# Layer 3's end: the last batch's chain woven with priority over the shared expert's rows and the first dense units

## The chip, the core and the metric

The kernel runs on one core of a Trainium2 chip. The metric is the device time of one execution in microseconds. The core's engines each work through a queue of their own, in order: TensorE (PE, matmuls), VectorE (DVE), ScalarE (ACT), GpSimd (POOL) and SyncE (SP, which only issues DMAs).

## What is computed

The reference is a decoder of four layers on x of shape (4, 512, 128), float32. Each layer adds a self-attention, a cross-attention and a feed-forward block to x, each with a layer norm before it. The change is in the last block, layer 3's mixture of experts:

```python
X = x.reshape(-1, D)                      # x after the layer norm, D = 128
scores = jax.nn.sigmoid(X @ gate_w.T)     # 32 experts
_, idx = jax.lax.top_k(scores + bias[None, :], K)          # K = 4
w = take(scores, idx); w = w / clip(sum(w), 1e-12)
pos = ...                                 # how many earlier tokens chose this expert
valid = pos < C                           # capacity of an expert, C = 128 over all 2048 tokens
h = silu(xe @ W1) * (xe @ W3); ye = h @ W2                 # per expert
out = sum over k of ye * w                # the dropped ones count 0
out = out + silu(X @ sw1.T) * (X @ sw3.T) @ sw2.T          # the shared expert
```

(Shortened here; in the reference C is worked out as 2 * T * K // E with T = 512, E = 32, which is 128. The kernel keeps one running count of choices over the four batches.)

## The kernel before

Tokens lie 128 to a tile, four tiles to a batch of 512. `x` holds the sum so far by rows, `xn` the normed rows, and `xT` the normed tokens turned, so that a batch is a 128x512 operand.

The kernel is written as Python generators whose steps are woven together by `Net.weave(dense, chain, every)`: after so many steps of the one, a step of the other is written. A planner then orders the instructions of each engine: among those that are ready, the one written first goes first. `high_priority(offset=n)` ranks the instructions written under it as if they had been written n places earlier. Stretches under `manual_schedule` keep the written order on the engines named. Tiles of one tag share a ring of buffers; in this stage TensorE writes into PSUM banks of the tags `f` (four), `acc` (one) and `s` (three).

The end of layer 3 goes like this. Batches 0 to 2 are routed during the cross-attention: their tokens are scattered into slots of their experts in DRAM by GpSimd's indirect DMAs (`put`, with a `pause` between two). Batch 3 is done in another way, densely: all experts see all its tokens. When the cross-attention is over, `add_columns(3)` adds its last sum onto x, and the stage of the change begins. It weaves two things:

- The dense side: `shared_rows` of batches 0, 1 and 2, two steps each. The first step writes the gate and the up product into two `f` banks (64 rows by 512), takes the silu on ScalarE (line 932) and the product on VectorE; the second step writes the down product into an `f` bank and adds it to x. After these come the first five steps of `dense_rows(3)`, which are units of experts for batch 3: gate and up products from `x3` into two `f` banks, silu (line 1065), product.
- The chain of batch 3: `norm(3)` (statistics and a reciprocal root on VectorE, lines 475 to 499; scaling on ScalarE, line 501; turning on TensorE, line 525; the copy to xT on ScalarE, line 526), `tokens_in_three` (xT as a sum of three bfloat16 parts, `x3`: a cast on ScalarE, line 732, the rest `x_rest` on VectorE, a second cast, line 735, and a difference), and `route_dense`, which is `capped` (router products and a sigmoid, line 594; the top four with max and match_replace; sums of weights; `before`, the counts of earlier choices; the places, lines 721 and 724) and then the weights split in three and turned into `w3T` (lines 747 to 756).

`w3T` is read by `weighted`, from the sixth dense step on. `widened` casts three packs of weights from bfloat16 to float32 (`w_wide`, lines 437 and 439); these are written before the weave. `slot_experts` follows: it fetches the slots of batches 0 to 2 from DRAM by eight DMAs on SP, computes the experts, and scatters the results back by 32 indirect DMAs on GpSimd. `returned` fetches these rows and adds them to x, and `store` writes the output.

In the stage before this one, the chains of batches 0 to 2 are woven with `ahead=300`; there, `weave` writes each step of a chain under `high_priority(offset=300)` until a step says "later".

Of the kernel before, what the change touches and what calls it, by code (L numbers as in the profile page):

```python
# [2340 lines left out]
def chained(*chains):  # L2341
    for c in chains:
        yield from c


def some(steps, n):

    for _ in range(n):
        if next(steps, steps) is steps:
            return  # L2350
        yield


def build(nc, packs, dram):
# [16 lines left out]
    with tile.TileContext(nc) as tc, ExitStack() as ctx:  # L2371
        net = Net(ctx, tc, packs, dram, feed)
# [96 lines left out]
        dense = lambda b: net.l2_dense(b, y[b], w4, s4)  # L2469
# [56 lines left out]
        shared = [net.shared_rows(b, net.stay[of("l3_ffn")[0]], ff) for b in range(3)]  # L2526
        chain = chained(net.norm(3), net.tokens_in_three(3, ff), net.route_dense(3, W5, s5))

        dense = net.dense_rows(3, ff)
        net.weave(chained(*shared, some(dense, 5)), chain, 0.3)  # L2530
        with tc.manual_schedule(engines={mybir.EngineType.Pool}):
            net.weave(net.slot_experts(at["l3"], ff), some(dense, 9), 3, 4)
        with tc.manual_schedule(engines={mybir.EngineType.DVE}):
# [28 lines left out]
```

## Time and profile before

| | us |
|---|---|
| median of 4 runs | 2147.36 |
| lowest and highest | 2143.18, 2151.99 |
| the profiled execution | 2143.46 |
| its span, first to last instruction | 2140.9 |
| TensorE busy | 2029.1 (95%) |
| VectorE, ScalarE, GpSimd busy | 1593.3, 989.6, 594.0 |
| mean granted TensorE clock | 0.984 |

Every time in a line of the profile is counted from the start of the span. A line of the timeline gives start, duration, engine, line of the code and operation with its output and inputs; in brackets stands how long the engine was idle before it and what released it. L431 is `dot` and L442 is `tt`, helpers through which most products and most two-operand steps of VectorE go; what they belong to is seen by the tile they write. The chain of waits is followed back from the last instruction, at each step to what released it. The granted clock is the share of its full speed that TensorE was allowed.

### The profile page before, as it was taken

Reading aid. Unit: us, or ns where it says so; the run is one execution under the profiler, and the core shown is the slowest. Engines: PE = TensorE matmul, PEld = TensorE weight load, DVE = VectorE, ACT = ScalarE, POOL = GpSimd, SP = SyncE. Lnnn points to the kernel's source line nnn. Section 1 sums busy time; section 2 is a strip of 40 time slices with the busy share of each in tenths; the row PEclk is TensorE's granted clock in tenths of the full one; section 3 lists DMA queues with packets and bytes.
Section 4 is the critical chain, followed back from the end, with each engine's and each line's share of the span. In section 5 each row is a group of like instructions: output and inputs, shape, how many; then the busy total and the mean of one; then the engine's idle time right before and its main releaser. Section 6 shows DMA issues by size and latency. Waiting matters only on the chain.

```text
span 2140.9 us, 27766 instructions
## 1 busy us (share of the span) xinstructions
PE 2029.1 (95%) x8804; PEld 1065.3 (50%) x8804; DVE 1593.3 (74%) x3932; ACT 989.6 (46%) x2023; POOL 594.0 (28%) x778
## 2 busy tenths in 40 slices
PE   6989999999999999999999999999999999899886
PEld 3556546554545453444444544444444444466553
DVE  6788665756775779788977798777866877599754
ACT  4566546444325462544543454434433544267541
POOL 2110001000000001433333243332433355245753
PEclk8999999999999999999999999999999999999998
DMA  6421443344453343343333444444454354431112
GB/s 162 122 78 47 107 113 101 93 130 112 118 137 89 93 105 99 89 104 97 102 103 106 111 112 127 123 134 115 127 135 119 98 141 124 96 99 36 32 43 82
DMA packets 93985, 222.56 MB, mean 104 GB/s; under 512 B 22178, under 2 KB 43106, under 8 KB 93582
## 3 DMA queue, kind: packets, MB, share of 16 engines
q1 hardware_dynamic: 90702, 218.63, 38.1%
q0 software_dynamic: 3136, 2.16, 0.4%
q8 instruction: 69, 1.13, 0.2%
q14 instruction: 78, 0.64, 0.1%
HBM read 192.55 MB, written 23.53 MB: 101 GB/s over the span
## 4 chain that ended last, share of the span: by engine, by line
PE 60%; DVE 13%; ACT 3%; issue 3%; POOL 2%; DMA 1%; another core or an unknown queue 0%; SPq 0%; DVEq 0%; POOLq 0%; ACTq 0%
PE mm L431 17%; PE f L431 11%; PE mm L1874 8%; PE s L431 6%; PE mm L1846 5%; PE acc L1039 5%; PE mm L1821 4%; DVE h L442 1%; DVE at_m L1907 1%; ACT at_e L1909 1%; DVE gvx L442 1%; PE acc L2326 1%; DVE k_work L442 1%; DVE og L442 1%; DVE x L442 1%
## 5 line engine op out<-in xcount | busy, mean ns | idle before, releaser
L1782 POOL TENSOR_TENSOR gvx<-gvx 128x512 f32<-128x512 f32 (+1 forms) x256 | 262.7, 1026 | 530.1 <-DVE gvx L442 471.7
L431 PE MATMUL f<-xT,w_l_ffn 128*128 128x512 f32 (+1 forms) x700 | 334.9, 599 | 1.3 <-ACT h L1031 0.7
L1909 ACT ACTIVATE at_e<-mm,at_m 128x512 f32<-128x512 f32 x256 | 173.1, 686 | 265.0 <-DVE at_m L1907 259.6
L431 PE MATMUL mm<-w_l_ffn_qkv,xT 128*128 128x512 f32 x512 | 264.4, 602 | 3.3 <-DVE gvx L442 1.7
L1874 PE MATMUL mm<-og,w_l_ffn_o 128*128 128x512 f32 x512 | 263.2, 600 | 2.8 <-DVE og L442 1.4
L442 DVE TENSOR_TENSOR h<-h,f 128x512 f32<-128x512 f32 (+1 forms) x175 | 119.4, 684 | 121.8 <-PE f L431 94.3
L1031 ACT ACTIVATE h<-f 128x512 f32<-128x512 f32 x172 | 102.2, 596 | 210.7 <-PE f L431 187.1
L442 DVE TENSOR_TENSOR gvx<-mm,gv 128x512 f32<-128x512 f32 x256 | 174.2, 684 | 23.7 <-PE mm L431 19.8
L442 DVE TENSOR_TENSOR og<-mm,c 128x512 f32<-128x512 f32 x256 | 174.1, 682 | 22.8 <-PE mm L1874 20.9
L431 PEld LDWEIGHTS f<-xT,w_l_ffn 128*128 128x128 f32 (+1 forms) x700 | 125.7, 190 | 130.2 <-issue 107.2
L1039 PE MATMUL acc<-h,w_l_ffn 128*128 128x512 f32 x344 | 176.7, 597 | 4.2 <-DVE h L442 2.9
L1907 DVE TENSOR_REDUCE at_m<-mm 128x1 f32<-128x512 f32 x256 | 161.2, 682 | 11.8 <-PE mm L431 11.2
L1822 ACT COPY eT<-mm 128x512 f32<-128x512 f32 x256 | 137.3, 595 | 68.4 <-PE mm L1821 68.0
L1821 PEld LDWEIGHTS mm<-ident,at_e 128*128 128x128 f32 x1024 | 119.4, 141 | 66.5 <-issue 45.4
L1874 PEld LDWEIGHTS mm<-og,w_l_ffn_o 128*128 128x128 f32 x512 | 91.3, 190 | 114.6 <-issue 90.7
L1821 PE MATMUL mm<-ident,at_e 128*128 128x128 f32 x1024 | 134.8, 273 | 3.3 <-ACT at_e L1909 3.3
L431 PEld LDWEIGHTS mm<-w_l_ffn_qkv,xT 128*128 128x128 f32 x512 | 86.9, 190 | 91.5 <-issue 54.5
L431 PE MATMUL mm<-roped 64*128 64x512 f32 x512 | 129.4, 615 | 1.6 <-DVE roped L442 1.6
L1846 PE MATMUL mm<-eT,v 128*64 128x512 f32 x512 | 118.5, 599 | 2.1 <-ACT eT L1822 2.1
L442 DVE TENSOR_TENSOR h<-h,c 128x512 f32<-128x512 f32 x160 | 111.1, 700 | 3.4 <-DMA c<-l_ffn_w 0.4
L1248 ACT ACTIVATE e<-mm 128x512 f32<-128x512 f32 (+1 forms) x176 | 92.1, 554 | 42.9 <-PE mm L1244 39.1
L1202 DVE TENSOR_REDUCE m<-mm 128x1 f32<-128x512 f32 (+3 forms) x176 | 102.7, 625 | 11.9 <-PE mm L1198 11.2
(528 smaller groups left out, 3481.4 us busy)
## 6 DMA issues: line engine op xcount, KB each, us to landing
c<-gates SPq DMA_DIRECT2D x256, 256.0 KB
c<-l_ffn_w SPq DMA_DIRECT2D x96, 384.0 KB
w_l_ffn_qkv<-in_l_ffn_qkv SPq DMA_DIRECT2D x24, 640.0 KB
w_l_ffn<-in_l_ffn SPq DMA_DIRECT2D x26, 576.0 KB
w_l_ffn_o<-in_l_ffn_o SPq DMA_DIRECT2D x24, 512.0 KB
rot<-qk SPq DMA_DIRECT2D x128, 64.0 KB
d<-inverted SPq DMA_DIRECT2D x64, 128.0 KB
k_parts<-k SPq DMA_DIRECT2D x12, 384.0 KB
```

The source lines that it names most:

```text
L431: self.nc.tensor.matmul(out, lhsT=lhsT, rhs=rhs, start=i == 0, stop=i == len(pairs) - 1)
L442: self.nc.vector.tensor_tensor(out, a, b, op)
L1031: nc.scalar.activation(h, pg, AF.Silu)
L1039: nc.tensor.matmul(acc["t"], lhsT=W["d" + u], rhs=h, start=i == 0, stop=i == n - 1)
L1202: nc.vector.tensor_reduce(m[:, i, h0 : h0 + per], ps, AX.X, ALU.max, negate=True)
L1782: nc.gpsimd.tensor_tensor(x[:, :, :m], x[:, :, :m], x[:, :, m : 2 * m], ALU.add)
L1821: nc.tensor.transpose(p[:, j, :], es[i][hl][:, j * P : j * P + P], self.ident)
L1822: nc.scalar.copy(eT[hl][:, :, i * P : i * P + P], p)
L1846: nc.tensor.matmul(po[64 * hl : 64 * hl + 64, :], lhsT=m["v"][:, j, hl, :], rhs=eT[hl][:, j, :], start=j == 0, stop=j == TB - 1,)
L1874: nc.tensor.matmul(acc, lhsT=W["o"][:, (e - 1) * D : e * D], rhs=hs.pop(e - 1), start=e == 1, stop=e == E)
L1907: nc.vector.tensor_reduce(m, s, AX.X, ALU.max, negate=True)
L1909: nc.scalar.activation(e[:, :n], s, AF.Exp, bias=m, accum_out=den)
```

## The change

One call gets one more argument:

```diff
         chain = chained(net.norm(3), net.tokens_in_three(3, ff), net.route_dense(3, W5, s5))
 
         dense = net.dense_rows(3, ff)
-        net.weave(chained(*shared, some(dense, 5)), chain, 0.3)
+        net.weave(chained(*shared, some(dense, 5)), chain, 0.3, ahead=300)
```

What `weave` does with it:

```python
while due >= every:
    with self.tc.high_priority(offset=ahead) if ahead and urgent else ExitStack():
        urgent = next(chain, None) != "later"
    due -= every
```

None of the steps of this chain says "later", so all steps that are written inside the loop over the dense side are ranked 300 places earlier. At 0.3, more than three steps of the chain are written after each step of the dense side. Instructions, operands and DMAs are the same as before; only their order on the engines can differ.

## The prediction

> **What bounds the kernel now.** I read the page first. TensorE is busy nearly all the time, and the chain that ended last runs through it.
>
> ```profile
> span 2140.9 us, 27766 instructions
> PE 2029.1 (95%) x8804; PEld 1065.3 (50%) x8804; DVE 1593.3 (74%) x3932; ACT 989.6 (46%) x2023; POOL 594.0 (28%) x778
> PE 60%; DVE 13%; ACT 3%; issue 3%; POOL 2%; DMA 1%; another core or an unknown queue 0%; SPq 0%; DVEq 0%; POOLq 0%; ACTq 0%
> ```
>
> That is an average over many stages. The change touches only the 29.4 us between the copy of the last attention sum (ends 2031.93) and the first slot product (2061.36), so I read the chain of waits there, in order of time (start, us, what):
>
> ```profile
> 2032.64 1.86 PE f L431 x4
> 2034.50 2.74 issue
> ...
> 2039.13 1.05 PE f L431 x2
> ...
> 2042.39 0.70 DVE x_rest L442
> 2043.73 5.67 PE f L431 x12
> 2049.40 2.02 PE s L431 x14
> ```
>
> Two things stand out. First, TensorE idles 2.74 us from 2034.50, although batch 1's gate product (tokens and weights long there) needs nothing from the norm; it starts only at 2039.06, after batch 0's down products. So the rows of the shared expert are a serial string, gate and up, silu, multiply, down, then the next batch, as they take the f banks in program order; the first dense unit (2052.96) follows batch 2's down. Second, from 2040.2 to 2043.73 the string waits for ScalarE and VectorE (the x_rest line is the last of that wait). The timeline of ScalarE there:
>
> ```profile
> 2040.20 0.59 ACT L526 COPY xT<-s 128x512 f32<-128x512 f32 x1 [1.87 <-PE f L431]
> 2040.69 1.16 ACT L439 CAST w_wide<-w_l_ffn 128x1152 f32<-128x1152 bf16 x1
> 2041.74 0.62 ACT L732 CAST x<-xT 128x512 bf16<-128x512 f32 x1
> 2042.26 0.59 ACT L932 ACTIVATE h<-f 64x512 f32<-64x512 f32 x1
> 2042.87 1.28 ACT L594 ACT_TABLE_LOAD   x1
> 2044.16 0.28 ACT L594 ACTIVATE sig<-s 128x128 f32<-128x128 f32 x1
> ```
>
> Batch 1's silu (L932) is ready at 2040.2 and runs at 2042.26, just ahead of the router's sigmoid. Third view: the stretches of 3.41 us (start:end, length, then busy time and count of PE, PEld, DVE, ACT, POOL; then PE clock):
>
> ```profile
> 2043.27:2046.69 3.42, 2.96 (x10) 2.12 (x11) 2.48 (x9) 2.94 (x4) 3.05 (x6) 0.50 0.01 0
> 2046.69:2050.10 3.41, 3.41 (x8) 1.18 (x6) 2.34 (x14) 0.59 (x1) 2.21 (x5) 0.50 0.03 3
> 2050.10:2053.51 3.41, 3.41 (x25) 2.85 (x25) 1.84 (x9) 0.00 (x0) 0.00 (x0) 1.00 0.63 189
> 2053.51:2056.92 3.41, 3.41 (x10) 1.25 (x8) 1.79 (x6) 0.90 (x2) 0.00 (x0) 0.50 0.99 355
> ```
>
> The granted clock is whole or half and changes on this grid. Half windows follow windows of idling or of many narrow products (the places' 128x32).
>
> **The change, part by part.** Nothing is added or removed; no DMA is issued by the moved steps. Every step of batch 3's chain (norm, three-part tokens, router, top four, places, turned weights) is put 300 places earlier in the planner's ranking, so wherever one of its instructions is ready it goes ahead of the shared rows, the weight casts (w_wide) and the dense units.
>
> What the chain's speed is worth: little. Its last product, w3T, is written at 2058.04 and first read at 2068.72; x3 is complete at 2045.77 and first read at 2052.96. Those 10.7 and 7.2 us of cover stand, so an earlier chain earns nothing itself. Norm on VectorE already runs without a foreign instruction between (2033.40 to 2036.65): zero there, and the 2.74 us stall stays. Pool has one memset of the chain and no other work of it; its queue is untouched. The slot fetches, on SP behind Pool's last scatter (2049.15), land by 2057.3: 4 us before their first reader, which covers a shift to earlier of that size.
>
> What it costs: places in the queues. ScalarE is a strict line. After xT (ends 2040.79) the ranking now prefers the cast to x (0.62, ends 2041.41). The shared silu stays behind the cast w_wide, which is ranked ahead of it as before (1.16, 2042.57). By then the second cast is ready (x_rest takes 0.69 from 2041.41), and so is the sigmoid, as the gate products (1.08) no longer wait for batch 1's up product. So: second cast 0.61 to 2043.18, table load 1.28, sigmoid 0.28 to 2044.74, table load back 1.28, silu 0.59 to 2046.61. Before, the silu ended at 2042.85: 3.76 later. The attention stage, where the other batches' chains have this same 300, shows such a double load: 1.28 at 2009.84, sigmoid 0.28, 1.28 at 2011.43, with the exponential behind them.
>
> The Trainium skill (ScalarE: Activation LUTs, What ACT_TABLE_LOAD costs) puts a switch at 2.66 us, 1.28 of load and 1.38 of drain. The rows show the 1.28 and no drain: the silu ends at 2042.85, the load starts at 2042.87, the sigmoid 0.01 after it. With the page's price the silu would be 2.8 later still; I go by the rows.
>
> VectorE's multiply (0.68) then meets the top four and the counts (sigmoid's sum to the last of them: about 3.7 us of work from 2044.74, so to 2048.5). It ends between 2047.29, if it finds a gap at once, and 2049.2, if it goes last. I take 2047.7, nearer the first, since those instructions depend on one another and leave gaps; before it ended at 2043.68. So 4.0 us later, and TensorE waits meanwhile: behind the missing down product, in the banks' order, stand batch 2's products and all dense units.
>
> From there TensorE works without a break. Before: 2043.73 to 2052.96, of which 6.37 at half clock, that is 3.19 + 2.86 = 6.05 us at full clock; then the dense units and w3T's turns to 2061.36, 0.55 + 1.70 + 4.44 = 6.69 at full clock. After, from 2047.7: half clock to 2050.10, since the window before is nearly empty (1.20 done, 4.85 left). If the next window is full, the dense units start at 2054.95, else at 2056.66. They end 6.69 later, or 1.70 more with one half window: 2061.64, 2063.34, 2063.35, 2065.05. Against 2061.36 that is +0.3, +2.0, +2.0, +3.7. I take +2.0.
>
> The Trainium skill (TensorE: Matmul & The Clock Gate, Part 1) says that about 3.4 us without work halves the clock and one busy window restores it; it warns of such gaps, and the change lengthens one. But 2050.10:2053.51 is busy throughout and is followed by a half window, so here products of little width count as idling. By the page alone the window after 2050.10 would be full and the sum +0.3.
>
> Behind 2061.36 everything moves along: slots, Pool's 32 scatters (1.27 us apart, none waited for at the end), the last products, the adds. One cover is uncertain: the chain of waits has three stalls of unknown origin there.
>
> ```profile
> 2091.19 4.23 another core or an unknown queue
> ...
> 2104.46 3.04 another core or an unknown queue
> 2107.66 2.67 another core or an unknown queue
> ```
>
> They sum to 9.9 us, more than any term above; they may grow or shrink by some us.
>
> The profiled execution took 2143.46 us (span 2140.9 and 2.6 around it), 3.9 below the median of the runs, 2147.36. +2.0 makes it 2145.5; on the median, 2149.4.
>
> **The rivals.** *The silu keeps its place* (0.25). If the gate products or the second cast are not ready when w_wide ends, batch 1's silu slips in as before. For it: sigmoid and silu now stand only one instruction apart. Then only the adds into x (0.69) and a multiply leave the chain's way, and nobody waits for the chain: -0.5. At best the gaps close and both groups of half windows vanish: 3.4 + 1.7 of half clock and the 1.73 wait at 2042.0, together -6.8.
>
> *The shared rows starve* (0.25), the slower side. If the multiply goes behind the last count, it ends at 2049.2. TensorE has done 0.45 by 2050.10; with two half windows (1.70 each) the remaining 2.2 end at 2059.1, the dense units at 2065.8 or, with one more half window, 2067.5: +4.4 to +6.1. Batch 2's multiply then meets the split of the weights (1.07): +6.5 in all. It decides from the point where the chain leaves no gap on VectorE; two parallel strings, counts and sums, speak for it, their waits for one another against it.
>
> *Absorbed later* (0.08): the three stalls shrink by what is lost: 0.
>
> **How the numbers follow.** Forecast 0.42: +2.0, 2149.4 us. A gap of 0.3% (6.4 us) is about what a measurement of this kernel can tell from no change. The forecast's own range, +0.3 to +3.7, stays within it; only the stalls or the spread of runs (2143.18 to 2151.99) carry it out. Slower by more: some 0.6 of the starving case, 0.2 of the forecast's: 0.25. Faster by more: a quarter of the silu case and a little of the rest: 0.10. Within: 0.65. The range takes -6 to +9.5 about the median: 2141.5 to 2157.
>
> **What would show it.** Right: sigmoid's table load before batch 1's silu on ScalarE; TensorE idle for 4 us or more about 2043 to 2047; x3 and w3T finished earlier; the first dense product later than 2052.96. Wrong: the silu still ahead of the sigmoid, or fewer half windows between 2037 and 2061, or batch 1's gate product starting before batch 0's down, which would break the serial string and make the stage shorter.

## The result and the profile after

The changed kernel takes 2153.15 us (median of 52 runs, 2142.76 to 2161.62) against 2147.38 us (78 runs, 2133.59 to 2158.55). The ratio of the runs is 1.0023, with a 95% interval of 1.0015 to 1.0032: about 5 us slower (3.2 to 6.9); the two medians are 5.8 us apart. The ratio lies within the 0.3% that the prediction set as its bound, though its interval reaches just beyond, and it is more than the +2.0 us forecast. In the experiments below, one of the twelve runs of `shared_too` took 3474.53 us, far above all others, and is not in its ratio.

The profiled execution of the changed kernel took 2162.78 us (span 2161.1), 9.6 us above its median, so it is not to be subtracted as a whole from the one before. It enters the stretch in question late: the copy of the last attention sum ends at 2042.30, 10.4 us later than before, in code that the change does not touch. Two lines of the page and its chain that ended last:

```profile
span 2161.1 us, 27767 instructions
PE 2046.1 (95%) x8804; PEld 1072.8 (50%) x8804; DVE 1592.8 (74%) x3932; ACT 989.8 (46%) x2023; POOL 592.7 (27%) x778
...
PE 60%; DVE 13%; ACT 3%; issue 3%; POOL 1%; DMA 1%; another core or an unknown queue 1%; SPq 0%; DVEq 0%; POOLq 0%; ACTq 0%
```

The page tells nearly nothing: the same shares, the same counts of instructions on all engines. The chain of waits in the stretch tells more (start, us, what):

```profile
2044.87 2.75 issue
2047.62 0.33 PE s L525
2047.95 0.41 PE f L431 x2
...
2052.18 1.28 ACT L594
2053.46 7.24 another core or an unknown queue
2060.70 0.27 ACT sig L594
...
2063.81 2.31 PE s L431 x10
...
2068.26 5.19 PE f L431 x10
...
2074.28 7.74 PE f L431 x38
```

The stall of 2.75 us is where it was. The turns of xn (L525) now alternate with batch 0's down products; the places' narrow products (2063.81) stand before batch 2's gate and up products; and there is something that no step of the prediction had, 7.24 us between the router's table load and its sigmoid. ScalarE's timeline shows the same:

```profile
2050.49 1.15 ACT L439 CAST w_wide<-w_l_ffn 128x1152 f32<-128x1152 bf16 x1
2051.54 0.62 ACT L732 CAST x<-xT 128x512 bf16<-128x512 f32 x1
2052.18 1.28 ACT L594 ACT_TABLE_LOAD   x1
2060.68 0.28 ACT L594 ACTIVATE sig<-s 128x128 f32<-128x128 f32 x1 [7.22 <-remote]
...
2061.48 1.28 ACT L932 ACT_TABLE_LOAD   x1
2062.77 0.59 ACT L932 ACTIVATE h<-f 64x512 f32<-64x512 f32 x1
```

Batch 1's silu (L932) stands behind the sigmoid and a second table load, as predicted. The sigmoid waits for the router's gate products alone. Their rows on TensorE end at 2054.20, and the counter that the sigmoid waits for steps, in the trace's semaphore events, only at 2060.65: the report that the products are done is 6.5 us late. (The profile models when a product ends, so a product that really ended later than its row would look the same; below, "late" means late by these rows.) "Remote" here is not another core but a report with no instruction ending near it.

The stretches on the grid of the clock, in this execution (start:end, length, busy time and count of PE, PEld, DVE, ACT, POOL, then PE clock):

```profile
2046.77:2050.19 3.42, 2.57 (x12) 1.73 (x12) 1.58 (x4) 1.83 (x5) 3.05 (x5) 1.00 0.04 8
2050.19:2053.60 3.41, 3.41 (x11) 1.61 (x10) 1.47 (x3) 3.25 (x4) 3.04 (x5) 0.50 0.02 1
...
2063.84:2067.25 3.41, 3.41 (x15) 3.12 (x15) 1.78 (x10) 0.00 (x0) 0.00 (x0) 0.50 1.01 340
```

The clock is half from 2050.19 to 2074.08, seven windows without a break; before there were three, not all adjacent. From the first slot product to the end both executions take the same: 79.55 us before, 79.21 after.

### The profile page after: what moved, and what is told of

It is laid out like the page before. It is cut to its first block, busy times and chain, and to the rows that moved or that the text cites. A ratio compares the mean times of both kernels' runs of the same rounds, so it can differ in the third digit from the quotient of the medians.

```text
span 2161.1 us, 27767 instructions
## 1 busy us (share of the span) xinstructions
PE 2046.1 (95%) x8804; PEld 1072.8 (50%) x8804; DVE 1592.8 (74%) x3932; ACT 989.8 (46%) x2023; POOL 592.7 (27%) x778
## 4 chain that ended last, share of the span: by engine, by line
PE 60%; DVE 13%; ACT 3%; issue 3%; POOL 1%; DMA 1%; another core or an unknown queue 1%; SPq 0%; DVEq 0%; POOLq 0%; ACTq 0%
PE mm L431 17%; PE f L431 11%; PE mm L1874 8%; PE s L431 6%; PE mm L1846 5%; PE acc L1039 5%; PE mm L1821 4%; DVE h L442 1%; DVE at_m L1907 1%; ACT at_e L1909 1%; DVE gvx L442 1%; DVE k_work L442 1%; PE acc L2326 1%; DVE og L442 1%; DVE x L442 1%
## 5 line engine op out<-in xcount | busy, mean ns | idle before, releaser
L1202 DVE TENSOR_REDUCE m<-mm 128x1 f32<-128x512 f32 (+3 forms) x176 | 102.7, 625 | 12.2 <-PE mm L1198 11.5
```

The lines of the kernel that those rows point to most:

```text
L1202: nc.vector.tensor_reduce(m[:, i, h0 : h0 + per], ps, AX.X, ALU.max, negate=True)
```

## The experiments

Three theories went in. A: what is lost is the wait for batch 1's silu behind the sigmoid and two table loads. B: the 7.2 us gap belongs to the new order. H, formed on the way: what is lost is half clock, because the new order leaves a window of the clock's grid of 3.41 us with narrow products only. "Wide" are the products of 128x512, "narrow" the turns (128x128), the down products (64x128) and those of the router and the places (128x32). "Stretch" is the time from the end of the sum's copy to the first slot product. All comparisons are with the kernel before on the same chip; the twelve runs came from three chips.

**The changed kernel again** (`after_again`). No edit.

> The changed kernel once more, nothing else, for a second profile of it. Theory A (the late silu): batch 1's shared silu stands behind the sigmoid and two table loads of 1.28 us, and that alone makes the stage longer. Then ScalarE runs the sigmoid at most about 1 us after its table load ends, the stretch from the last attention sum's copy to the first slot product is 31 to 34 us (29.4 before), and the ratio is 1.001 to 1.003. Theory B (the stall): the 7.2 us that ScalarE stood still between the table load and the sigmoid in the first profile belong to the new order and come back in every run. Then the stall of 6 to 8 us is there again and the stretch is 38 to 41 us; as the median lies only 5 us up, B also needs something of 3 to 5 us that is saved elsewhere. If the stall is an accident of one execution, it is absent or in another place.

Measured: 1.0031 (1.0008 to 1.0053). The gap is there again, 7.17 us; stretch 39.46 us, 39.55 in the first profile. At that point B looked right, and the order of the queues was the thing to vary.

**The shared rows get the same priority** (`shared_too`).

```
-shared = [net.shared_rows(b, W, ff) for b in range(3)]
+shared = [urged(net.shared_rows(b, W, ff), tc) for b in range(3)]   # each step under offset=300
```

> The changed kernel, and the rows of the shared expert get the same priority of 300 as the norm, router and places. Among themselves they then keep their written order; only the weight casts and the dense units are outranked. On ScalarE both remaining shared silus stand ahead of the sigmoid. Theory A: the loss goes away with the silu's place, ratio 0.997 to 1.000 (stretch 27 to 29.5 us). Theory B: the stall goes with the sigmoid's table load, which is still there; but the shared rows no longer wait for it, so 0 to +3 us, ratio 1.000 to 1.0015. A third theory, C: the priority over the dense units and the casts is what costs, not that over the shared rows; then it stays at about 1.0023.

Measured: 1.0001 (0.9984 to 1.0018), stretch 31.06 us. The loss is gone, or at least most of it, and C's 1.0023 lies outside the interval. Both remaining silus stand ahead of the sigmoid, which A wanted; but the gate and up products of batch 1, which are wide, now stand among the turns and the down products too, and half clock begins one window later:

```profile
2037.40:2040.81 3.41, 2.57 (x9) 1.25 (x10) 2.24 (x5) 2.44 (x6) 3.17 (x3) 1.00 0.04 8
2040.81:2044.23 3.42, 2.75 (x11) 1.37 (x10) 1.37 (x2) 2.00 (x3) 2.87 (x7) 1.00 0.01 0
2044.23:2047.64 3.41, 3.41 (x8) 1.35 (x7) 0.69 (x1) 1.10 (x3) 2.98 (x6) 0.50 0.02 1
```

Once begun, it lasts four windows, longer than in the first profile of before (three). So this run tells A from H no further.

**Priority for the norm and the three-part tokens alone** (`norm_first`). The steps of `route_dense` yield "later", which takes the priority from them.

```
-chained(net.norm(3), net.tokens_in_three(3, ff), net.route_dense(3, W5, s5))
+chained(net.norm(3), net.tokens_in_three(3, ff), plain(net.route_dense(3, W5, s5)))
```

> Only the norm and the three-part tokens get the priority of 300; router, top four, places and turned weights keep the old rank. Of all queues only TensorE's differs from the kernel before: the four turns of xn and batch 0's four down products alternate instead of standing in two groups. Theories A and B: no loss, ratio 0.9985 to 1.001. If the norm's priority is what costs: 1.0015 to 1.003.

Measured: 1.0015 (0.9997 to 1.0033), the lower end of what was expected if the norm's priority costs, and above what A and B expected; the interval reaches into both and decides nothing. The profile does more. The order on ScalarE and VectorE is that of the kernel before, instruction by instruction; only the alternation of turns and down products on TensorE differs. The same two windows of the grid, first in the kernel before, then here:

```profile
2036.45:2039.86 3.41, 2.62 (x14) 1.74 (x15) 2.61 (x6) 1.65 (x4) 3.04 (x5) 1.00 0.03 5
2039.86:2043.27 3.41, 2.14 (x11) 1.10 (x9) 1.17 (x3) 3.05 (x5) 3.04 (x5) 1.00 0.02 1
```

```profile
2036.38:2039.80 3.42, 2.55 (x12) 1.71 (x12) 1.60 (x4) 1.81 (x5) 3.05 (x5) 1.00 0.04 8
2039.80:2043.21 3.41, 3.41 (x6) 0.76 (x5) 2.19 (x3) 2.10 (x4) 3.23 (x5) 0.50 0.02 1
2043.21:2046.62 3.41, 2.57 (x18) 2.10 (x18) 0.68 (x1) 1.76 (x2) 2.85 (x7) 1.00 0.02 0
```

TensorE is about as busy in the first window of each (2.62 and 2.55 us), and half clock follows only where no wide product is in it. The silu is ahead of the sigmoid here, and the gap before the sigmoid is there too (4.52 us). That is against B.

**Priority for the router, places and turned weights alone** (`route_first`).

```
-chained(net.norm(3), net.tokens_in_three(3, ff), net.route_dense(3, W5, s5))
+chained(plain(net.norm(3)), net.tokens_in_three(3, ff), net.route_dense(3, W5, s5))
```

> Only the router, top four, places and turned weights get the priority of 300, the norm and the cast to three parts keep the old rank. On ScalarE the sigmoid then stands ahead of the cast to x and of batch 1's silu, so sigmoid and silu are a cast and a table load apart as in the changed kernel. Theory A: the whole loss is here, ratio 1.0015 to 1.003, stretch 31 to 34 us. Theory B: the stall of some 7 us between table load and sigmoid is here too. If neither part alone costs, 0.9985 to 1.001.

Measured: 1.0018 (1.0001 to 1.0034), stretch 34.07 us, the gap before the sigmoid 0.70 us, a gap of 2.70 us before xT instead. Not B's 7 us, though sigmoid and silu stand as B wants them. By the ratios either part of the priority costs a little, 0.15% and 0.18%; the intervals are too wide to split the loss between them, and the first reaches below no loss at all. Half clock is four windows here, the turns stand together as in the kernel before, and most of the longer stretch is TensorE's idling behind the late report.

**Without batch 2's scatters, before and after** (`quiet_before`, `quiet_after`).

```
 while net.puts:
-    net.put(1)
+    net.puts.pop(0)
     net.pause()
```

> The kernel before without the 16 scatters of batch 2 into the slots (their rows are left out of the slots; the pauses between them stay), so that Pool issues nothing in the stretch from the last attention sum's copy to the first slot product. A control for the next one. If scatters hold back what TensorE reports as done (theory P), the xT copy comes some 1 us earlier after the last turn of xn than the 1.07 us of before, and the stretch is 27.5 to 29.4 us. If not, 29 to 30 us. The slots' reads start earlier in any case.

> The changed kernel without the same 16 scatters. The stall of 7.2 us came back in the second profile of the changed kernel, so it is no accident; the sigmoid's only wait is for the gate products, whose rows end 6.5 us before it. Theory P: the signal that they are done is late because Pool issues scatters; without them the sigmoid follows its table load within 1 us, the stretch is 31 to 34 us, and the ratio to the control is 1.000 to 1.002. Theory Q: TensorE's own order (the gate products between narrow K=64 products, or the table load) makes the signal late; then the stall of 6 to 8 us stays, the stretch is 38 to 41 us and the ratio to the control 1.002 to 1.005.

Measured: 1.0001 (0.9985 to 1.0016) and 1.0027 (1.0009 to 1.0046) against the kernel before; against one another 2135.78 to 2129.03, 1.0032 or 6.75 us. Neither profile has a late report. But that does not speak for P: this chip had none in the next two kernels either, which keep the scatters, so the question whether scatters delay the reports could not be put here. What the pair gives is better than that: the change's effect with no gap in either profile, 26.34 against 32.98 us of stretch, +6.6, as much as the medians differ. (The profiled execution of the changed one is 5.25 us above its median; it enters the stretch 5.8 us later than the control's, in code that is the same.) The order on TensorE, ScalarE and VectorE is in `quiet_after` that of the changed kernel, instruction by instruction. First the control's TensorE and then the changed order's, up to the first wide product (line, operation, tiles, shape, count):

```profile
2037.76 0.33 PE L525 MATMUL s<-ident,xn 128*128 128x128 f32 x1 [2.68 <-ACT xn L501]
2038.02 1.16 PE L431 MATMUL f<-w_l_ffn,h 64*128 64x128 f32 x8
2039.11 0.55 PE L525 MATMUL s<-ident,xn 128*128 128x128 f32 x3
2039.58 1.93 PE L431 MATMUL f<-xT,w_l_ffn 128*64 128x512 f32 x4
```

```profile
2043.59 0.33 PE L525 MATMUL s<-ident,xn 128*128 128x128 f32 x1 [2.68 <-ACT xn L501]
2043.85 0.48 PE L431 MATMUL f<-w_l_ffn,h 64*128 64x128 f32 x2
...
2045.87 0.49 PE L431 MATMUL f<-w_l_ffn,h 64*128 64x128 f32 x2
2046.28 1.97 PE L431 MATMUL f<-xT,w_l_ffn 128*64 128x512 f32 x2
```

From the first turn to the wide product it is 1.82 us in the control and 2.69 in the other: alternating, each turn meets a pair of down products, the narrow work drags on, and the first wide product (128x512) falls just behind the edge of the window instead of inside it. The windows of the two, control first:

```profile
2037.01:2040.43 3.42, 2.67 (x14) 1.75 (x15) 2.73 (x5) 2.39 (x6) 0.00 (x0) 1.00 0.03 5
...
2050.67:2054.08 3.41, 3.41 (x10) 1.17 (x8) 2.12 (x6) 0.60 (x1) 0.00 (x0) 0.50 0.00 0
```

```profile
2042.80:2046.22 3.42, 2.63 (x12) 1.73 (x12) 1.52 (x4) 1.90 (x5) 0.00 (x0) 1.00 0.02 5
2046.22:2049.63 3.41, 3.41 (x11) 1.74 (x9) 2.05 (x3) 3.19 (x4) 0.00 (x0) 0.50 0.00 0
2049.63:2053.04 3.41, 2.37 (x5) 0.62 (x4) 2.35 (x16) 2.66 (x4) 0.00 (x0) 0.50 0.00 0
2053.04:2056.46 3.42, 3.19 (x13) 2.94 (x14) 2.01 (x11) 0.00 (x0) 0.00 (x0) 0.50 0.01 2
2056.46:2059.87 3.41, 3.41 (x13) 2.76 (x14) 1.86 (x6) 0.00 (x0) 0.00 (x0) 0.50 0.00 0
2059.87:2063.28 3.41, 3.41 (x8) 0.91 (x6) 0.62 (x3) 0.59 (x1) 0.00 (x0) 0.50 0.00 0
```

The first line of each is the same window of the stretch, with TensorE as busy (2.67 and 2.63 us). The one with 0.85 us of wide products in it is followed by full clock, the one without by half, and there it stays for five windows: the first two of them hold 1.97 us of wide products each, at half speed, and the next two mostly the narrow places and down products; the one filled by batch 2's wide products (3.03 us) and the turned weights (2059.87) ends it. The control has one half window, behind the places.

The other profiles agree. In seven of the fourteen (`quiet_after`, `after`, `after_again`, `norm_first`, `lagged_before`, `after_same`, `silu_first`) the window of the turns holds turns and down products only, with TensorE busy for 2.5 to 2.7 us, and half clock follows in all seven. In five (`before`, `quiet_before`, `shared_too`, `route_first`, `dense_between`) 0.7 to 1.3 us of wide products stand in it too, TensorE is no busier, and full clock follows in all five. How much wide work a window needs is not found: in the kernel before, 2039.86:2043.27 has 1.1 us of it beside the router's narrow products and half clock follows, and in `shared_too` 2040.81:2044.23 has 0.85 us and half clock follows too. In the last two profiles, `oneset_after` and `before_same`, the grid lies elsewhere: an edge falls 2.9 us after the sum's copy, in the other twelve 1.0 to 1.1 us.

**No table loads around the router** (`oneset_after`). A silu stands for the sigmoid of layer 3's last batch.

```
-nc.scalar.activation(m["sig"], ps, AF.Sigmoid)
+nc.scalar.activation(m["sig"], ps, AF.Silu if group == (3,) and E == 32 else AF.Sigmoid)
```

> The changed kernel with a silu in place of the sigmoid of layer 3's last batch (other routing weights for that batch, the same instructions otherwise), so that both table loads of 1.28 us go and the order of all queues stays. Theory A (the silu is late because of the table loads): it starts 2.6 us earlier, the stretch shrinks by 2.5 to 3 us, ratio 1.000 to 1.0015. Theory P: the late signal covers the first load, only the second is saved; the gap before the activation is 8 to 9 us instead of 7.2, the stretch shrinks by 1 to 1.5 us, ratio 1.0015 to 1.003. If the table load itself causes the late signal, the gap is under 2 us and the ratio 0.998 to 1.000.

Measured: 1.0043 (1.0029 to 1.0057). The ratio lies above all three expectations, so by the runs nothing is won back. But the test is not as clean as it was meant to be. Both loads are gone, yet the order of the queues did not stay: batch 1's silu now stands ahead of the second cast, its multiply ahead of the top four, and batch 2's wide products ahead of the places. ScalarE waits for TensorE:

```profile
2038.67 0.28 ACT L594 ACTIVATE sig<-s 128x128 f32<-128x128 f32 x1 [2.31 <-PE s L431]
2038.85 0.58 ACT L932 ACTIVATE h<-f 64x512 f32<-64x512 f32 x1
```

The gate products are late here: the clock is half from 2031.82 on, because in this execution the early wait falls into one window of the grid (0.90 us busy). The stretch is 30.80 us, 2.2 less than in `quiet_after`, while the median is higher; the profiled execution is 11.5 us below its own median. So this run does not settle A by itself, and why its median is the highest on this chip stays open.

**The string of the shared rows broken** (`lagged_before`), in the kernel before: gate and up of the next batch are written ahead of the down products of the one before.

```
-net.weave(chained(*shared, some(dense, 5)), chain, 0.3)
+go = lambda b: next(shared[b], None)
+rows = net.lagged([(b,) for b in range(3)], (go, 0), (go, 1))
+net.weave(chained(rows, some(dense, 5)), chain, 0.3)
```

> The kernel before with the string of the shared rows broken: the gate and up products of the next batch are written ahead of the down products of the one before. TensorE's wait of 2.74 us for xn is then partly filled with batch 1's 1.7 us, and batch 1's silu runs before the norm's activations. If the string is what binds this stretch, it shrinks by 1.5 to 3.5 us and the ratio is 0.998 to 0.9995. If the late signals bind it (gate products, turns of xn), nothing is gained or 1 to 4 us are lost, as more of the string stands behind them: 1.000 to 1.002.

Measured: 1.0024 (1.0002 to 1.0045), the opposite of what was expected of the string, and without a late report. Batch 1's wide products now fill the early wait, where the clock is full anyway; the window of turns and down products is left narrow, and half clock lasts six windows. H explains it, by the same reading as in the pair. A does not: batch 1's silu ends 6.88 us after the sum's copy, against 9.82 us in `quiet_before`.

**Before and after on a third chip** (`before_same`, `after_same`). No edits.

> The kernel before, unchanged, for its profile beside those of the next three on one chip. In four of the runs so far no signal of TensorE came late and the times were 18 us lower throughout, so the late signals may belong to a chip and not to a kernel. With late signals: stretch 29.4 us as in the first profile; without: 26 to 28 us, as in the control without scatters (26.3). Ratio 0.999 to 1.001.

> The changed kernel, unchanged, on the same chip. With late signals: a gap of some 7 us between table load and sigmoid, stretch 39 to 40 us in the profile. Without: gap under 1 us, stretch 32 to 34 us. In both cases the ratio is 1.002 to 1.0035, if what is lost is the idling of TensorE behind batch 1's silu and the half clock after it.

Measured: 1.0008 (0.9990 to 1.0025) for the control, 1.0028 (1.0007 to 1.0049) for the changed kernel. The stretches in the profiles, 38.20 and 36.88 us, are not the ones expected. The profile of the kernel before is the one that ends theory B:

```profile
2039.24 0.59 ACT L932 ACTIVATE h<-f 64x512 f32<-64x512 f32 x1
2039.85 1.28 ACT L594 ACT_TABLE_LOAD   x1
2048.61 0.28 ACT L594 ACTIVATE sig<-s 128x128 f32<-128x128 f32 x1 [7.47 <-PE f L431]
```

The old order, silu in its old place, and the sigmoid waits 7.47 us all the same (3.72 in the changed kernel's profile of this call). In this pair of profiles the kernel before even has the longer stretch, while its median is 3.6 us lower. Two things differ from its first profile. TensorE idles for 9.20 us instead of 4.52, behind the late reports; and the clock's grid lies otherwise, so that a whole window falls into the early wait:

```profile
2031.46:2034.88 3.42, 0.83 (x6) 0.71 (x7) 3.05 (x12) 1.37 (x4) 3.05 (x5) 1.00 0.02 3
2034.88:2038.29 3.41, 3.41 (x11) 1.73 (x10) 1.40 (x2) 1.38 (x3) 2.85 (x7) 0.50 0.04 5
```

In this profile the old order has six half windows as well. A single profile with late reports, or with another lie of the grid, does not stand for a kernel.

**Only the silu and the multiply first** (`silu_first`).

```
+with self.tc.high_priority(offset=400):
     nc.scalar.activation(h[:H], pg[:H], AF.Silu)
     self.tt(h[:H], h[:H], pu[:H], ALU.mult)
```

> The changed kernel, and only the silu and the multiply of the shared rows get a still higher priority (400). Batch 1's silu is then ahead of the cast to x and of the sigmoid, its multiply ahead of the three-part subtraction, and the down products of batch 1 stand ahead of the places again; batch 2's multiply stays behind the top four, and the turns of xn still alternate with batch 0's down products. Theory A (the late silu is the loss): -0.5 to +1.5 us, ratio 0.9985 to 1.0007. Theory H (the alternating narrow products let a window of the clock count as idle, and the half clock that follows is the loss): the clock is half from the gate products on, stretch 3 to 5 us over that of before, ratio 1.0012 to 1.0025.

Measured: 1.0021 (1.0003 to 1.0038), as much as the change itself, in H's band; A's lies mostly outside the interval, though not wholly. (The stretch, 37.17 us, has late reports in it and can't be held against H's 3 to 5 us.) ScalarE has the order that A wanted, and it does not help, because the silu now waits for TensorE at half clock:

```profile
2042.33 0.59 ACT L933 ACTIVATE h<-f 64x512 f32<-64x512 f32 x1 [2.63 <-PE s L431]
2042.82 0.60 ACT L732 CAST x<-xT 128x512 bf16<-128x512 f32 x1
2043.44 1.28 ACT L594 ACT_TABLE_LOAD   x1
2048.05 0.28 ACT L594 ACTIVATE sig<-s 128x128 f32<-128x128 f32 x1 [3.32 <-remote]
```

**Dense units between the shared rows** (`dense_between`), in the kernel before, as a version that might beat both.

```
-chained(*shared, some(dense, 5))
+chained(shared[0], net.turns(chained(*shared[1:]), some(dense, 5)))
```

> The kernel before with another written order: the steps of the shared rows of batches 1 and 2 alternate with the first dense units, so that wide products stand between gate and down of a batch and between the places. If the waits of the serial string and the half clock of narrow products are what this stretch loses, it shrinks by 2 to 4 us and the ratio is 0.998 to 0.9993. If TensorE then waits for the tokens in three parts instead (complete 13.8 us after the sum's copy in the kernel before), nothing is gained: 0.9993 to 1.001.

Measured: 0.9998 (0.9976 to 1.0019), stretch 30.54 us with a late report of 4.17 us before xT in it. Half clock is three windows, as in the first profile of before, and no gain can be told. No version tried beats the kernel before.

**The sum over the profiles.** The stretch from the sum's copy to the first slot product is TensorE's idle time, plus its busy time, of which half is lost wherever the clock is half. Worked out from the instructions and the clock's windows of each profile (us):

| kernel | stretch | idle | lost to half clock | rest | slot product to end |
|---|---|---|---|---|---|
| before | 29.43 | 4.52 | 4.88 | 20.03 | 79.55 |
| after | 39.55 | 10.76 | 8.06 | 20.73 | 79.21 |
| quiet_before | 26.34 | 4.35 | 1.71 | 20.28 | 67.57 |
| quiet_after | 32.98 | 4.29 | 7.90 | 20.79 | 67.56 |
| lagged_before | 33.45 | 4.52 | 8.51 | 20.41 | 67.57 |
| shared_too | 31.06 | 3.41 | 6.83 | 20.82 | 80.82 |
| norm_first | 35.90 | 6.68 | 8.51 | 20.72 | 79.36 |
| silu_first | 37.17 | 8.68 | 7.32 | 21.16 | 81.80 |
| after_again | 39.46 | 10.74 | 7.98 | 20.73 | 79.28 |
| route_first | 34.07 | 8.71 | 5.07 | 20.30 | 78.60 |
| oneset_after | 30.80 | 3.78 | 6.41 | 20.62 | 67.57 |
| before_same | 38.20 | 9.20 | 9.47 | 19.54 | 82.59 |
| after_same | 36.88 | 8.36 | 7.73 | 20.79 | 82.21 |
| dense_between | 30.54 | 6.27 | 4.50 | 19.77 | 81.60 |

The rest, 19.5 to 21.2 us, is the same work in every order. In the pair without gaps the idle time is the same to 0.1 us, and 6.2 of the 6.6 us are half clock. Between the first two rows, half clock is 3.2 us of the 10.1, idle time 6.2, most of it the late report. That the clock is the cause is read from orders that moved it, and from this sum; the clock itself was not held fixed in any run. The pair shows it where no report is late and the grid lies alike. On the other two chips the profiles can't split the 5 us: the kernel before loses 4.88 us to half clock in one and 9.47 in the other, the changed one 7.7 to 8.1.

## Why the prediction was right or wrong

**The place and the pass-through: right.** Only the stretch was touched, and what lies behind it passes the shift on: in each pair of profiles (before and after, `before_same` and `after_same`, the two quiet ones) the time from the first slot product to the end is the same to 0.4 us, and to 0.01 us in the pair without late reports.

**An earlier chain earns nothing: not tested, since the chain did not come earlier.** The prediction named "x3 and w3T finished earlier" among its signs of being right. They finish later: counted from the sum's copy, x3 is complete after 12.74 us in the control of the quiet pair and after 13.41 in the changed order, w3T after 23.02 and 25.74; in the first pair of profiles it is 13.84 and 19.98, 26.11 and 32.35. The sigmoid waits for gate products that run at half clock (in the quiet pair it ends after 12.08 us instead of 11.41). What does hold is the cover: x3's first reader comes later still (17.94 and 26.49 us), so x3's lateness by itself costs nothing.

**Norm "zero there": this step failed.** The prediction looked at VectorE, where nothing changes, and not at the other queue that the norm's last step uses. Its four turns on TensorE go through the same ranking; each is now taken as soon as its quarter of xn is ready, between pairs of batch 0's down products. That costs no TensorE work, but it pushes batch 1's wide gate product over the edge of a window (by 0.06 us in `quiet_after`), and half clock follows; `norm_first`, where nothing else is moved, shows it. A list of every instruction of the norm that is ranked anew, queue by queue, would have had these four.

**The order on ScalarE: right, with one slip.** The sigmoid's table load is ahead of batch 1's silu, w_wide still ahead of both. The second cast went behind the sigmoid, not before it, as it had stood in the kernel before (2044.33, behind 2044.16). Without a gap the multiply ends 15.80 us after the sum's copy (predicted: 2047.7 - 2031.93 = 15.77) and the silu 14.48 us after it (predicted 14.68).

**The 4.0 us for which "TensorE waits meanwhile": wrong in kind.** In the quiet pair TensorE's idle time did not grow (4.35 and 4.29 us). The wait is filled by gate products and batch 1's up product at half clock, and by the places, which the prediction left behind batch 2's products. The silu is 4.7 us later in the pair (3.76 in the sum). That its place is not what is lost is read from `silu_first`, where it is in front again and the time is lost all the same (1.0021), and from `lagged_before`, which loses as much with the silu early (1.0024). Both intervals are wide, and `oneset_after` can't tell what the table loads alone cost.

**The clock: the term that was mis-sized.** The sum let half clock start at 2043.27 as before and allowed one more half window, 1.7 us at most. Measured: from one to five half windows in the pair, 6.2 us. The prediction knew that the places' narrow products count as idling; it did not apply this to the turns and the down products. The Trainium skill (TensorE: Matmul & The Clock Gate, Part 1) has the clock fall after an idle window of some 3.4 us and rise after a busy one. The pair's rows differ from it on both counts: 2042.80:2046.22 is 2.63 us busy and half clock follows, while the control's 2.67 us keeps full clock; and 2056.46:2059.87 is busy throughout and full clock does not follow. The measurement decides: what products are in a window counts, wide ones or narrow ones, not only that TensorE is busy.

**The rivals.** The measured +5 lies beyond the forecast's own +0.3 to +3.7 and inside the starving rival's +4.4 to +6.5; the interval, 3.2 to 6.9, touches both. The rival's mechanism is not there: batch 1's multiply stands behind one count, not behind the last, much as the forecast had it, and batch 2's, though it stands behind the split of the weights, finds VectorE idle for 2.79 us before it in `quiet_after` and waits for TensorE. So the rival's size came about by another way, half clock. The silu did not keep its place. The stalls of unknown origin were rightly named as the uncertain cover; they turned out to reach into the stretch itself, before and after alike.

**The numbers.** 2153.15 lies in the range (2141.5 to 2157.0), and a change within 0.3% was the likeliest outcome given. That the time lies in it is luck in part: what kept the time in the range was the width given for unknown stalls and the spread of runs, not the sum, whose way of losing time is not the one that the runs show.

## What to carry to other kernels

When a step is moved up in a planner's ranking, list its instructions on every queue, those on TensorE too: four turns that changed places cost nothing in work, and with the places moved too the new order lost 6 us to the clock. Count, for each window of the clock's grid, how much wide work is left in it; in the pair, a window that just lost its one wide product was followed by five at half clock. Look also at where the grid lies in each profile: two of fourteen had it elsewhere, and with it other half windows. And where a wait's releaser is unknown, take a second profile of the unchanged kernel before blaming the change.

## What the runs showed of the hardware that was not expected

TensorE's reports of finished products can come some us after the end of the products' rows: 6.5 us for the gate products in the first profile of the changed kernel, 3.7 to 7.5 us of gap before the sigmoid on the third chip in both kernels. On the second chip the chain of waits has none in any of the four profiles, and it is there that the kernel before takes 2129.55 us instead of 2147.51 and 2152.33. The whole difference lies behind the sum's copy, from which on the four profiles take 94 to 101 us, and those of the other two chips 109 to 121. All gaps in the profiles of the first and third chip fall in stretches where Pool issues scatters or has just ended, none where it is quiet; but the second chip has none with scatters either. What delays the reports, and why not on that chip, stays open.
